# Layer 0 of a four-layer image network: Silu built from exp and ln, and its steps laid into separate slots

## The chip, the cores and the metric

The kernel runs on one core of a Trainium2 chip. The metric is the device time of one execution in microseconds (us). The core has five engines that run side by side: TensorE (PE, with its weight loads shown apart as PEld), VectorE (DVE), ScalarE (ACT), GpSimd (POOL) and the DMA queues (issued here by SP). Each engine works through its own instructions in order and waits for the others through semaphores.

## The reference

Four layers work one after the other on four images of 64 x 64 positions with 128 channels; each adds its result to its input. Only layer 0 is changed. Cut to what matters:

```python
xz = gn(x) @ in_proj_w.T                    # 128 -> 512 channels
xh, z = jnp.split(xz, 2, axis=-1)           # 256 each
z = jax.nn.silu(z)                          # silu(v) = v / (1 + exp(-v))
xc = depthwise_conv_3x3(xh)
xc = jax.nn.silu(xc + conv_b)
xs = [xc by rows, xc by columns, and both reversed]          # 4 directions
delta = softplus(dt_proj(x_proj(xs)) + dt_bias)              # ln(1 + exp(.))
for t in range(4096):                                        # 16 states n per channel
    h[n] = exp(delta[t] * A[n]) * h[n] + delta[t] * xs[t] * B[t, n]
    y[t] = sum_n h[n] * C[t, n]
y = sum over the 4 directions, plus D * xs
y = layernorm(y) * out_norm_w + out_norm_b
x = x + (y * z) @ out_proj_w.T
```

Layers 1 to 3 (Fourier layers and a neighbourhood attention) follow and are the same in both kernels.

## The kernel before

Layer 0 works image by image. An image has four directions of eight chunks (512 positions each), which makes 32 units; a unit has 16 slots, one for each state n. In a slot GpSimd makes dB = du * B, ScalarE makes dA = exp(delta * A) for the two halves s of the channels, VectorE runs the recurrence as two scans h, and TensorE transposes the h of seven slots earlier into pt; ScalarE copies that to hT, and TensorE multiplies it with W (made from C) into yT. During an image's units two further stages are fed piece by piece into the slots: `before` of the next image (norm, in_proj, conv, Silu) and `after` of the last image (layer norm, gate, out_proj, residual). The first image's `before` runs ahead of all units, as the opening, in an order that the compiler's scheduler chooses; in the units the written order is kept. The last image's `after` follows at the end.

```python
psx = pool("l0psx", 3, space=PSUM)      # 3 banks of dA, tag "x"
psm = pool("l0psm", 1, space=PSUM)      # 1 shared bank, tag "m"
exp_and_ln = lambda: nc.scalar.preload_act_table_set("natural_log_exp_and_others")
...
def before(b, bank, act, dve):
    ...                                 # 8 pieces: transposes and statistics of x
    s_, o_ = sh.group_scale(st, psm, small, "m")     # has a Sqrt
    exp_and_ln()
    for c in range(NCH):
        ...                             # transposes, norm into xn; in_proj xh, copied into pad
        for s in range(2):
            for t in range(9):
                if t % 3 == 0:
                    yield "c"
                if t == 0:
                    pm = bank("cv")
                dy, dx = divmod(t, 3)
                nc.tensor.matmul(pm, lhsT=taps[:, s, t, :],
                                 rhs=pad[:, s, dy : dy + 8, dx : dx + 64], ...)
            zp = psx.tile([P, CH], F32, name="zp", tag="x")
            nc.tensor.matmul(zp, lhsT=w_in[:, 2 + s, :], rhs=xn[:, o : o + CH], ...)
            act(lambda *a: gates(b, *a), c, s, pm, zp)

def gates(b, c, s, pm, zp):
    xo = tmp.tile([P, CH], F32, name="xo", tag="t2", bufs=4)
    nc.scalar.activation(xo, pm, AF.Silu, bias=conv_b[:, s : s + 1])
    ...                                 # DMA to xr
    xw = tmp.tile([P, 64, 8], F32, name="xw", tag="t2", bufs=4)
    nc.scalar.activation(xw, pm.rearrange("p (h w) -> p w h", w=64), AF.Silu, bias=...)
    ...                                 # DMA to xw
    z = tmp.tile([P, CH], F32, name="z", tag="t2", bufs=4)
    nc.scalar.activation(z, zp, AF.Silu)
    exp_and_ln()
    ...                                 # DMA to z
```

The slot loop, cut; `flush(act)` runs what a piece of an earlier slot has left for ScalarE, `flush(dve)` what it has left for VectorE:

```python
for n in range(NS):
    dB = ...;  nc.gpsimd.tensor_tensor(dB, du, B_now[...], ALU.mult)
    flush(dve)
    for s in range(2):
        dA = psx.tile([P, CH], F32, name="dA", tag="x")
        nc.scalar.activation(dA, delta[:, s, :], AF.Exp, scale=A_neg[:, k, s, n : n + 1])
        nc.vector.tensor_tensor_scan(h[:, s, :, q], dA, dB[:, s, :], state[...], ALU.mult, ALU.add)
        if s == 0:
            flush(act)
            ...                         # exp and ln of the next unit's delta at n = 8, 10
    copy = transposed()                 # PE: pt, then yT of the slot before
    copy()                              # ACT: hT <- pt
    if n in CRS:                        # CRS = {2: 0, 4: 1, 11: 2, 13: 3}
        cr = spare("cr");  nc.tensor.matmul(cr, ...);  defer(dve)(weights, ...)   # W <- cr
    ...
    # one piece of `before` or `after`; conv pieces start at n == 14 and go on in the next two slots
```

Of the kernel before, what the change touches and what calls it, by code (L numbers as in the profile page):

```python
# [16 lines left out]
P = 128  # L17
# [64 lines left out]
def layer0(sh, A, x_in, x_out, scr):  # L82
# [7 lines left out]
    with ExitStack() as ctx:  # L90
# [16 lines left out]
        on_w, on_b = cols[:, 28:30], cols[:, 30:32]  # L107
        w_x = wp.tile([P, 2, K4, 40], F32, name="w_x")
# [32 lines left out]
        def before(b, bank, act, dve):  # L141
# [4 lines left out]
            for c in range(NCH):  # L146
                yield "f"
                t = tmp.tile([P, 4, DM], F32, name="xs", tag="t2", bufs=4)
                nc.sync.dma_start(t, tiles(x_in(b)[c * CH : (c + 1) * CH, :]))
                yield "m"  # L150
                pt = bank("gn_ps")
                for q in range(4):
                    nc.tensor.transpose(pt[:, q * P : (q + 1) * P], t[:, q, :], sh.ident)
                dve(lambda c=c, pt=pt: nc.vector.bn_stats(st[:, c, :], pt))
# [3 lines left out]
            for c in range(NCH):  # L158
# [13 lines left out]
                for j in range(0, j1 - j0, 3):  # L172
# [3 lines left out]
                    for q in range(j, e):  # L176
                        nc.tensor.transpose(pt[:, (q - j) * P : (q - j + 1) * P], t[:, q, :], sh.ident)
                    dve(
                        lambda j=j, e=e, pt=pt: nc.vector.tensor_scalar(  # L179
                            xn[:, j * P : e * P], pt[:, 0 : (e - j) * P], s_, o_, ALU.mult, ALU.add  # L180
                        )
                    )
                for s in range(2):
                    for r in range(r0, r1, 5):
# [8 lines left out]
                        act(  # L193
                            lambda s=s, p0=p0, n=n, pm=pm: nc.scalar.copy(
                                pad[:, s, p0 : p0 + n, 1:65], pm[:, 0 : 64 * n].rearrange("p (h w) -> p h w", w=64)
                            )
                        )
                o = (8 * c - 2 * j0) * 64
                for s in range(2):
                    for t in range(9):  # L200
# [12 lines left out]
                    zp = psx.tile([P, CH], F32, name="zp", tag="x")  # L213
                    nc.tensor.matmul(zp, lhsT=w_in[:, 2 + s, :], rhs=xn[:, o : o + CH], start=True, stop=True)
                    act(lambda *a: gates(b, *a), c, s, pm, zp)

        def gates(b, c, s, pm, zp):

            xo = tmp.tile([P, CH], F32, name="xo", tag="t2", bufs=4)
            nc.scalar.activation(xo, pm, AF.Silu, bias=conv_b[:, s : s + 1])  # L220
            nc.sync.dma_start(scr(f"xr{b % 2}")[s, :, c * CH : (c + 1) * CH], xo)
            xw = tmp.tile([P, 64, 8], F32, name="xw", tag="t2", bufs=4)
            nc.scalar.activation(xw, pm.rearrange("p (h w) -> p w h", w=64), AF.Silu, bias=conv_b[:, s : s + 1])
            nc.sync.dma_start(scr(f"xw{b % 2}")[s].rearrange("p (w h) -> p w h", h=64)[:, :, 8 * c : 8 * c + 8], xw)
            z = tmp.tile([P, CH], F32, name="z", tag="t2", bufs=4)
            nc.scalar.activation(z, zp, AF.Silu)
            exp_and_ln()
            nc.sync.dma_start(scr(f"z{b % 2}")[s, :, c * CH : (c + 1) * CH], z)

        def after(b, st, bank, act, dve):  # L230
# [8 lines left out]
            for c in range(NCH):  # L239
# [3 lines left out]
                nc.sync.dma_start(y, tiles(scr("y2")[rows, :]))  # L243
                z = tmp.tile([P, 2, CH], F32, name="zf", tag="t4", bufs=4)
                nc.sync.dma_start(z, scr(f"z{b % 2}")[:, :, rows].rearrange("s p t -> p s t"))
# [8 lines left out]
                for s in range(2):  # L254
                    yield "m"
                    pt = bank("pg")
                    for q in range(4):
                        nc.tensor.transpose(pt[:, q * P : (q + 1) * P], y[:, q, s * P : (s + 1) * P], sh.ident)
                    act(
                        lambda s=s, yg=yg, pt=pt: nc.scalar.activation(  # L260
                            yg[:, s, :], pt, AF.Identity, scale=on_w[:, s : s + 1], bias=on_b[:, s : s + 1]
                        )
                    )
# [4 lines left out]
                yield "m"  # L268
                op = bank("op").rearrange("p (q d) -> p q d", q=4)
# [5 lines left out]
                dve(lambda *a: residual(b, *a), rows, xr, op)  # L275
# [53 lines left out]
        at_once = lambda f, *a: f(*a)  # L329
        for _ in before(0, any_bank, at_once, at_once):  # L330
# [88 lines left out]
        CRS = {2: 0, 4: 1, 11: 2, 13: 3}  # L419
        BUSY = (*CRS, 6, 7, 8, 9, 10)  # L420
        act, dve = [], []
        defer = lambda todo: (lambda f, *a: todo.append(lambda: f(*a)))

        def flush(todo):
            for f in todo:
                f()
            todo.clear()
# [10 lines left out]
        with tc.manual_schedule(engines=order):  # L438
            for i, (b, k, c) in enumerate(units):
                if i % per == 0:  # L440
                    ln_st = small.tile([P, NJ, 1, 6], F32, name="ln_st")
                    if b + 1 < NB:
                        sides.insert(0, Side(before(b + 1, spare, defer(act), defer(dve)), 113 + 8, NS * i, 29 * NS))
                rev = k >= 2
                pc = NCH - 1 - c if rev else c
                dst = lambda n, pc=pc: tiles(scr(f"y{n}")[pc * CH : (pc + 1) * CH, :])
# [7 lines left out]
                for n in range(NS):  # L454
                    g, q = divmod(n, 4)
# [10 lines left out]
                    flush(dve)  # L466
                    if i + 1 < len(units) and n in (9, 11):
                        next(coming)
                    for s in range(2):
# [5 lines left out]
                        if s == 0:  # L475
                            flush(act)
                            if i + 1 < len(units):
                                if n == 7:
                                    xd_next, bd_next = next(coming)
                                if n in (8, 10):  # L480
                                    next(coming)
                    copy = transposed() if NS * i + n >= LAG else (lambda: None)
                    copy()
                    if n == 1:
                        for f in ends.pop("state", []):
                            f()
                    if n in CRS:
                        cr = spare("cr")
                        nc.tensor.matmul(cr, lhsT=sel[:, CRS[n], :], rhs=xd[0:40, :], start=True, stop=True)  # L489
                        defer(dve)(weights, Ws, CRS[n], int(rev), cr)  # L490
# [11 lines left out]
                    if i + 1 < len(units):  # L502
                        if n == 3:
                            u_next, v_next = fetch(*units[i + 1])
                        if n == 6:
                            coming = inputs(*units[i + 1][1:], v_next)
                        if n in (6, 7, 9):
                            next(coming)
                        if n == 13:
# [11 lines left out]
                    holds = any(d.inside or d.run for d in sides)  # L521
# [1264 lines left out]
```

## Time and profile before

| | |
|---|---|
| time, median of 3 runs | 8981.49 us (8977.56 to 8983.19) |
| span of the profiled execution | 9002.5 us |
| PE / DVE / ACT / POOL busy over the span | 81% / 78% / 70% / 62% |
| opening, to the first scan | 222 us |
| images 0, 1, 2, 3 in the scan | 1592, 1618, 1618, 1447 us |
| ACT loads of a table of functions, in front of xo and by exp_and_ln | x49 and x58, 1283 ns each |
| scan h, 128x512 | x4096, mean 1270 ns |
| dA, 128x512 | x4096, mean 690 ns |
| hT <- pt, 128x1024 | x2048, mean 1011 ns |
| dB, 128x1024 | x2048, mean 2378 ns |

A line of the groups names the source line, the engine, the operation, the tile written and those read, the shapes and the count; then come the busy time, the mean of one, and the idle time of the engine just before it with what ended it. A line of the waits names who waited for whom, with the sum, the count and the longest. A line of the timeline gives start and length in us. Overlapping instructions of one engine are each counted from their own start to their own end, so that the mean of one can be somewhat longer than its share of the time.

### The profile page before, as it was taken

To read this page: it belongs to the slowest core of one execution; us is meant where nothing else is said; L and a number is where in the kernel's file an instruction comes from. 1 tells how busy PE (TensorE), PEld (TensorE's weight loads), DVE (VectorE), ACT (ScalarE), POOL (GpSimd) and SP (SyncE) were. 2 spreads that over 40 slices of the span, in tenths; PEclk is the share of its full clock that TensorE was granted. 3 is DMA by queue.
4 is the path that set the end of the run, shared out by engine and by line. 5 is a ranking of instruction groups with operands and counts; after the bars stand their busy time and mean duration, and the time that the engine had idled before them with its cause. 6 is when DMAs were issued, how large, how long until landed. Compare 5 with 4: busy or idle time off the path is not lost. (4 is left out here: it accounts for less than half of the span.)

```text
span 9002.5 us, 141536 instructions
## 1 busy us (share of the span) xinstructions
PE 7279.6 (81%) x54256; PEld 4342.6 (48%) x54256; DVE 6999.1 (78%) x8298; ACT 6266.3 (70%) x9869; POOL 5607.3 (62%) x2998
## 2 busy tenths in 40 slices
PE   8788888878888887888888778887768968488588
PEld 3344444444444444444444444444457745365366
DVE  1788888998889899898888999999824543534578
ACT  2788888888788788887888888888712212515467
POOL 0788888888878788887878888999700010110233
PEclk9799999999999999999999999999979978688699
DMA  6234544434454443444545333444341033240333
GB/s 108 99 121 138 132 124 141 126 122 133 129 135 139 138 131 118 128 135 123 147 138 135 123 122 136 146 139 140 111 104 47 24 93 100 75 118 30 90 90 87
DMA packets 1148650, 1037.91 MB, mean 115 GB/s; under 512 B 564127, under 2 KB 1001979, under 8 KB 1081156
## 3 DMA queue, kind: packets, MB, share of 16 engines
q1 hardware_dynamic: 1146292, 1027.13, 39.3%
q8 instruction: 426, 6.98, 0.3%
q14 instruction: 252, 2.06, 0.1%
q10 hardware_dynamic: 1680, 1.74, 0.1%
HBM read 845.18 MB, written 181.32 MB: 114 GB/s over the span
## 5 line engine op out<-in xcount | busy, mean ns | idle before, releaser
L465 POOL TENSOR_TENSOR dB<-du,Bb 128x1024 f32<-128x1024 f32 x2048 | 4841.1, 2378 | 974.4 <-DVE h L472 554.1
L472 DVE TENSOR_TENSOR_SCAN h<-dA,state,dB 128x512 f32<-128x512 f32 x4096 | 4972.6, 1270 | 507.3 <-ACT dA L471 428.8
L358 PE MATMUL pt<-ident,h 128*128 128x128 f32 x16384 | 2319.7, 287 | 868.2 <-ACT hT L368 856.5
L471 ACT ACTIVATE dA<-delta,A_neg 128x512 f32<-128x512 f32 x4096 | 2757.5, 690 | 250.3 <-DVE h L472 221.4
L358 PEld LDWEIGHTS pt<-ident,h 128*128 128x128 f32 x16384 | 1872.4, 145 | 2067.6 <-ACT hT L368 1744.5
L368 ACT COPY hT<-pt 128x1024 f32<-128x1024 f32 x2048 | 2070.6, 1011 | 540.4 <-PE pt L358 526.9
L393 PE MATMUL yT<-hT,W 128*32 128x256 f32 x16384 | 1364.2, 406 | 3.9 <-DVE y L409 3.3
L489 PE MATMUL cr<-xd,sel 40*128 40x512 f32 x1024 | 611.3, 678 | 39.1 <-DVE delta L310 20.3
L206 PE MATMUL cv<-pad,taps 128*128 128x512 f32 x1152 | 536.5, 606 | 7.3 <-DVE W L431 6.6
L393 PEld LDWEIGHTS yT<-hT,W 128*32 128x32 f32 x16384 | 328.3, 110 | 364.7 <-issue 351.2
L855 POOL TENSOR_TENSOR xg<-xg,so 128x1024 f32<-128x1024 f32 x8 | 26.5, 3337 | 695.4 <-ACT so L855 674.4
L1504 POOL TENSOR_TENSOR S<-S,sm 128x784 f32<-128x784 f32 x128 | 191.4, 1495 | 403.3 <-DVE sm L1502 341.7
L431 DVE TENSOR_TENSOR W<-cr,diag 128x512 f32<-128x512 f32 x512 | 343.5, 671 | 57.6 <-PE cr L489 57.0
L304 PE MATMUL dp<-xd,w_dt 65*128 65x512 f32 x512 | 294.7, 658 | 70.4 <-DVE delta L310 69.8
L313 POOL TENSOR_TENSOR du<-delta,u 128x1024 f32<-128x1024 f32 x128 | 304.4, 2378 | 73.3 <-DVE delta L310 73.3
L206 PEld LDWEIGHTS cv<-pad,taps 128*128 128x128 f32 x1152 | 206.0, 189 | 275.6 <-issue 259.6
L855 POOL TENSOR_TENSOR z<-z,sp 128x1024 f32<-128x1024 f32 x16 | 41.9, 2617 | 475.9 <-ACT z L855 475.6
L489 PEld LDWEIGHTS cr<-xd,sel 40*128 40x128 f32 x1024 | 160.5, 196 | 275.0 <-issue 134.0
L294 PE MATMUL xd_ps<-u,w_x 128*40 128x512 f32 x512 | 251.0, 613 | 40.9 <-DVE xn L179 21.1
L1511 ACT ACTIVATE S<-S,mx 128x196 f32<-128x196 f32 x512 | 228.2, 449 | 33.7 <-DVE mx L1538 33.3
L855 PE MATMUL pz<-PT,WX 128*68 128x64 f32 x2048 | 163.3, 244 | 94.4 <-DVE WX L855 76.6
L855 POOL TENSOR_TENSOR WX<-wr,Xs 128x544 f32<-128x544 f32 x32 | 45.1, 1408 | 269.4 <-DMA wr<-wt 239.4
(333 smaller groups left out, 7888.9 us busy)
## 6 DMA issues: line engine op xcount, KB each, us to landing
Bb<-l_B SPq DMA_DIRECT2D x512, 1024.0 KB
l_y<-y SPq DMA_DIRECT2D x128, 512.0 KB
wr<-wt SPq DMA_DIRECT2D x256, 136.0 KB
u<-l_xw SPq DMA_DIRECT2D x64, 512.0 KB
y<-l_y SPq DMA_DIRECT2D x64, 512.0 KB
u<-l_xr SPq DMA_DIRECT2D x64, 512.0 KB
V<-l_v SPq DMA_DIRECT2D x512, 49.0 KB
l_xr<-xo SPq DMA_DIRECT2D x64, 256.0 KB
```

The costliest lines, as they stand in the source:

```text
L206: nc.tensor.matmul(pm, lhsT=taps[:, s, t, :], rhs=pad[:, s, dy : dy + 8, dx : dx + 64], start=(t == 0), stop=(t == 8),)
L304: nc.tensor.matmul(dp, lhsT=w_dt[:, k, s * P : (s + 1) * P], rhs=xd, start=True, stop=True)
L313: nc.gpsimd.tensor_tensor(du, delta, u, ALU.mult)
L358: nc.tensor.transpose(pt[:, j, s, :], G["h"][:, s, t0 : t0 + 32, :].rearrange("p t n -> p (t n)"), sh.ident)
L368: return lambda: nc.scalar.copy(hT, pt.rearrange("p j s d -> p j (s d)"))
L393: nc.tensor.matmul(U["yT"][e][32 * jo : 32 * jo + 32, qo % 2, :], lhsT=U["Ws"][G["g"]][:, 4 * q + j, :], rhs=hT[:, j, :], start=((e, jo) n ...
L431: nc.vector.tensor_tensor(W, cr.rearrange("p (a t) -> p a t", t=32), diag[:, rev : rev + 1, :].to_broadcast([P, 16, 32]), ALU.mult,)
L465: nc.gpsimd.tensor_tensor(dB, du, B_now[:, q : q + 1, :].to_broadcast([P, 2, CH]), ALU.mult)
L471: nc.scalar.activation(dA, delta[:, s, :], AF.Exp, scale=A_neg[:, k, s, n : n + 1])
L472: nc.vector.tensor_tensor_scan(h[:, s, :, q], dA, dB[:, s, :], state[:, s, n : n + 1], ALU.mult, ALU.add)
L489: nc.tensor.matmul(cr, lhsT=sel[:, CRS[n], :], rhs=xd[0:40, :], start=True, stop=True)
L855: r = f(*args, **kw)
```

## The change

Silu has a set of functions of its own in ScalarE's tables, and exp and ln are in another, which must be loaded again afterwards. The changed kernel computes silu(v) as v * exp(-ln(1 + exp(-v))): exp, ln and exp on ScalarE from the set that the scan uses anyway, and a product on VectorE. The two copies of the conv's Silu, by rows and by columns, are now one Silu and a copy of it. Work left over by a piece gets a place in a given later slot: "dve" at its start, "act0" and "act1" behind the first and the second dA, "act2" behind the copy of pt. The z matmul gets a piece of its own ("z", at n = 12), two slots ahead of its group's conv.

As the shared bank is now held longer by conv and z, the matmuls of `after` (pg and op) take a bank of dA, in pieces "x" at n = 4, 6, 8 or 10, and the slots of cr and of the inputs of the next unit move. Scratch z has three copies instead of two and y2 two instead of one, so that `after` may spread over 28 units instead of 22.

```diff
-                    zp = psx.tile([P, CH], F32, name="zp", tag="x")
-                    nc.tensor.matmul(zp, lhsT=w_in[:, 2 + s, :], rhs=xn[:, o : o + CH], start=True, stop=True)
-                    act(lambda *a: gates(b, *a), c, s, pm, zp)
 (ahead of the conv of the same s)
+                    yield "z"
+                    zp = bank("zp")
+                    nc.tensor.matmul(zp, lhsT=w_in[:, 2 + s, :], rhs=xn[:, o : o + CH], start=True, stop=True)
+                    silu(zp, 0.0, 0.0, scr(f"z{b % 3}")[s, :, c * CH : (c + 1) * CH], later, (0, 0, 1))
 (behind the conv)
+                    bias = conv_b[:, s : s + 1], conv_nb[:, s : s + 1]
+                    xo = silu(pm, *bias, scr(f"xr{b % 2}")[s, :, c * CH : (c + 1) * CH], later, (0, 1, 2))
+                    later("act0", by_columns, xo, scr(f"xw{b % 2}")[s], c, slots=4)
...
-        def gates(b, c, s, pm, zp):      (three Silus and exp_and_ln, shown above)
+        def silu(v, bias, minus, dst, later, wait):
+            e = tmp.tile([P, CH], F32, name="e", tag="t2", bufs=4)
+            def product():
+                nc.vector.scalar_tensor_tensor(e, v, bias, e, ALU.add, ALU.mult)
+                nc.sync.dma_start(dst, e)
+            later("act0", nc.scalar.activation, e, v, AF.Exp, scale=-1.0, bias=minus)
+            later("act1", nc.scalar.activation, e, e, AF.Ln, bias=1.0, slots=1 + wait[0])
+            later("act0" if wait[1] else "act2", nc.scalar.activation, e, e, AF.Exp, scale=-1.0, slots=1 + wait[1])
+            later("dve", product, slots=1 + wait[2])
+            return e
+        def by_columns(xo, dst, c):
             xw = tmp.tile([P, 64, 8], F32, name="xw", tag="t2", bufs=4)
+            nc.scalar.copy(xw, xo.rearrange("p (h w) -> p w h", w=64))
...
 (in after; op likewise)
-                    yield "m"
-                    pt = bank("pg")
+                    yield "x"
+                    pt = psx.tile([P, CH], F32, name="pg", tag="x")
...
-        CRS = {2: 0, 4: 1, 11: 2, 13: 3}
-        BUSY = (*CRS, 6, 7, 8, 9, 10)
+        CRS = {3: 0, 4: 1, 10: 2, 11: 3}
+        BUSY = (*CRS, 5, 6, 7, 8, 9)
...
-                    sides.insert(0, Side(before(...), 113 + 8, NS * i, 29 * NS))
+                    sides.append(Side(before(...), 17 + 8 * 15, NS * i, 29 * NS))
...
-                sides = [Side(after(...), 4 + 8 * 6, NS * (i + 1) + 8, 22 * NS)]
+                sides = [Side(after(...), 4 + 8 * 7, NS * (i + 1) + 8, 28 * NS)]
```

In the opening, `later` runs each step where it is written, and all banks, zp's too, come in turn from the three of dA and the shared one.

## The prediction

> **What bounds the kernel now.** I first cut the span into stretches, at the scans that begin each image of layer 0, and asked for the busy time of every engine in each: opening, images 0 to 3, and the tail of image 3. The columns are stretch and length, then PE, PEld, DVE, ACT and POOL busy (instructions), then clock and DMA.
>
> ```profile
> 0.00:222.00 222.00, 181.35 (x476) 85.51 (x476) 25.25 (x60) 60.02 (x100) 7.03 (x27) 0.93 0.62 109
> 222.00:1814.00 1592.00, 1333.29 (x9192) 713.68 (x9192) 1389.56 (x1321) 1330.45 (x1836) 1298.10 (x680) 0.94 0.44 126
> 1814.00:3432.00 1618.00, 1354.20 (x9490) 736.75 (x9490) 1447.29 (x1400) 1327.34 (x1847) 1315.73 (x687) 0.96 0.46 132
> 3432.00:5050.00 1618.00, 1356.94 (x9490) 738.19 (x9490) 1447.71 (x1400) 1328.13 (x1847) 1315.62 (x687) 0.96 0.46 132
> 5050.00:6497.00 1447.00, 1163.44 (x9016) 647.07 (x9016) 1417.73 (x1367) 1244.00 (x1725) 1306.24 (x665) 0.97 0.38 132
> 6497.00:6615.00 118.00, 59.70 (x300) 44.42 (x296) 21.59 (x80) 22.02 (x26) 18.73 (x8) 0.63 0.33 102
> ```
>
> The last image, which prepares no next image, is bound by VectorE: 1417.73 of 1447 us. Images 1 and 2 have only 30 us more VectorE work but take 171 us more; VectorE stands idle there for 1618 - 1447 = 171 us each (202 in image 0). The list of VectorE's waits within 222 to 6497 says on whom:
>
> ```profile
> DVE h L472 <- ACT dA L471: 428.8, 334, 4.6
> DVE W L431 <- PE cr L489: 57.0, 50, 1.8
> ```
>
> So the loss is exponentials (dA) that come late from ScalarE. The timeline around one of the 48 conv groups inside the scan shows why (start, length, engine, instruction, idle time before it and its releaser):
>
> ```profile
> 4137.09 2.84 PE L206 MATMUL cv<-pad,taps 128*128 128x512 f32 x6
> ...
> 4138.38 2.46 DVE L472 TENSOR_TENSOR_SCAN h<-dA,state,dB 128x512 f32<-128x512 f32 x2 [1.07 <-POOL pad L166]
> ...
> 4141.30 2.84 PE L206 MATMUL cv<-pad,taps 128*128 128x512 f32 x6
> 4141.81 0.70 ACT L471 ACTIVATE dA<-delta,A_neg 128x512 f32<-128x512 f32 x1
> ...
> 4142.52 1.28 ACT L220 ACT_TABLE_LOAD   x1
> 4142.60 1.28 DVE L472 TENSOR_TENSOR_SCAN h<-dA,state,dB 128x512 f32<-128x512 f32 x1 [1.77 <-ACT dA L471]
> ...
> 4144.18 0.69 ACT L220 ACTIVATE xo<-cv,cols 128x512 f32<-128x512 f32 x1 [0.38 <-PE cv L206]
> ...
> 4145.95 1.28 ACT L119 ACT_TABLE_LOAD   x1
> ...
> 4147.25 0.69 ACT L471 ACTIVATE dA<-delta,A_neg 128x512 f32<-128x512 f32 x1
> ...
> 4147.97 1.28 DVE L472 TENSOR_TENSOR_SCAN h<-dA,state,dB 128x512 f32<-128x512 f32 x1 [4.09 <-ACT dA L471]
> ...
> 4148.94 1.43 PE L358 MATMUL pt<-ident,h 128*128 128x128 f32 x8 [2.49 <-ACT hT L368]
> ```
>
> Two losses sit side by side. The conv's three pieces of 2.84 us stretch three slots to the 4.2 us that TensorE needs (start to start of these two pieces: 4141.30 - 4137.09), against some 2.7 without them (1447/512 = 2.83 is the mean slot of image 3, with its other work). Then load, three Silus and load keep dA away from 4142.51 to 4147.25. After it TensorE is slow: the transposes take 1.43 us here and 1.97 us two slots on, against 1.04 before. Over all 48 groups, from the starts of the scans in the trace, the slots from one before the loads to two after take 18.5 us, and the same four slots of image 3 take 10.6: 7.9 us per group, 127 us per image. That is most of the 171.
>
> **What the Trainium skill says.** "ScalarE: Activation LUTs", section "What ACT_TABLE_LOAD costs", gives about 1283 ns for a load and 1380 ns more for a drain. The trace agrees on the load (1.28 us) but shows no second part: the load at 4145.95 ends at 4147.23 and dA starts at 4147.25. I count 1.28. The same page, "Table sets: the hidden batching unit", says that natural_log_exp_and_others holds both exp and ln; after the first few units the trace indeed has no load between the two activations of delta. "TensorE: Matmul & The Clock Gate", section "What's actually happening", says an idle window of about 3.4 us halves the clock. The 2.49 us gap above, shorter than that, already comes with longer matmuls, so the tendency agrees and the threshold isn't confirmed.
>
> **The change, part by part.**
>
> *Removed in the scan.* 48 groups lose two loads (48 x 2 x 1.28 = 123 us of ScalarE) and three Silus (688 + 681 + 598 ns in the groups by form, 1.97 us each group).
>
> *Added in the scan.* Each group gets six activations of about 0.6 us (the exp and ln of delta, same shape, are 596 and 632 ns) and one copy of about 0.6: 4.2 us. That is no less than the 4.5 removed; the gain must come from the spread. VectorE gets two products of 663 ns (the row of delta's SCALAR_TENSOR_TENSOR): 1.3 us per group, 64 us in all.
>
> *The group replayed by hand*, on the timeline above. The conv ends at about 4144.0, as before, so the waits of 1.07 and 1.77 stay. exp (0.69) runs from 4144.2 and dA follows at 4144.8, ends at 4145.5: the scan waits 1.6 us and not 4.09. ln, then the copy of the transposes, then dA of the next slot end at 4147.6: another 0.9 us. The second exp hides. At the end of slot 2 I am at 4150.1 and before was at 4152.0. The product adds 0.66. Before, the next W then waited 1.4 us for a slowed cr matmul (2.07 us for the two); that wait goes. At the first scan of the next slot: before 4154.0, after 4150.75 plus one W of 0.67, so 2.6 us gained. The z chain, three activations in slot 13, costs ScalarE 1.85 us where it has 0.4 to 1.2 idle per slot; its product falls into waits that the conv makes anyway. I charge 0.2. **Net 2.4 us per group, 115 us for 48.**
>
> *Opening.* Here the change adds loads. In the instruction order of the changed kernel on ScalarE, 64 loads stand in the opening, each ln and each exp after it bringing its own set: the preload after the group scale has no instruction that depends on it and no longer stands in front of them. The kernel before has one load for all Silus there. Per chunk: four chains of 0.6 + 1.28 + 0.63 + 1.28 + 0.6 = 4.4 us, two copies and four pad copies (2.0): 20.8 us of ScalarE. TensorE needs 21.06 us per chunk (conv to conv: 55.63, 76.69 in the timeline of xo) and was nearly alone:
>
> ```profile
> 55.63 0.69 ACT L220 ACTIVATE xo<-cv,cols 128x512 f32<-128x512 f32 x1 [7.59 <-PE cv L206]
> ...
> 76.69 0.69 ACT L220 ACTIVATE xo<-cv,cols 128x512 f32<-128x512 f32 x1 [7.66 <-PE cv L206]
> ```
>
> Now the pad copies of a chunk stand behind the last chain of the chunk before, about 6 us after its conv, and one xh matmul waits for the bank which that chain holds until its product. The next conv starts about 8 us after the last instead of 4, and starts with a slowed TensorE, about 1 us more. 5 us x 8 chunks = 40, plus the longer last chain before the first fetch: **+43 us.** Further, 16 loads in the first units of image 0 (8 in front of ln, 8 in front of dA) stay as they are.
>
> *The later stage.* pg and op take dA's banks, 24 times an image in three images. For one slot dA then has two banks and not three; one dA takes 0.69 us and a scan 1.2, so two are enough. The opposite sign is possible too, since pg no longer waits for the single shared bank. I count 0. In the tail (118 us, 8 chunks) the second pg no longer waits 0.8 us for the first: **-6 us.** The third z and the second y2 only widen the time in which the stage may run; VectorE shows no wait for these transfers, so 0.
>
> Sum: -115 + 43 - 6 = -78; 8981 - 78 = 8903, rounded to 8905.
>
> **The rivals.** (a) *All of the gate was a stall*: the 7.9 us per group shrink to the conv's own 3 or so, and two products are hidden: about 4.5 us per group, -216, net 8800. For it: nearly all of VectorE's idle time names dA. Against it: dA behind a conv is late through TensorE too. (b) *VectorE becomes the payer*: its 64 us of products add in full, and spread activations still delay dA, since ScalarE has just 0.45 us of slack in a 2.7 us slot (two dA and a copy, 2.25). Then 0 to -40 in the scan, the opening costs 43, and the total is 8980 to 9025. For it: image 3 is 98% VectorE. Against: in the group's slots VectorE is the one that waits. (c) *The opening is worse*, with ScalarE at 20.8 us per chunk as the bound and TensorE cold at every start: +70 and not 43. (d) *dA's lost bank bites*: 72 uses x 0.7 us = 50 us in images 1 to 3. Image 3 alone would show it.
>
> **Range and chances.** The scan's term has the width: -40 to -200. The opening is +25 to +70. 8810 to 8990 holds most combinations. Faster by over 2% (under 8802) needs rival (a) whole: 0.11. Slower by over 2% (over 9161) needs something I don't see: 0.03. Within 2%: 0.86.
>
> **What would show it.** Opening: first scan at about 265 us instead of 222, with 64 loads on the line of the new calls. Images 1 and 2: about 1580 us each instead of 1618, VectorE busy about 20 us more, its wait for dA near 300 us instead of 429. Image 3 unchanged at 1447 within 10 (else rival d). Loads in the scan: 8 + 8 + 6 pairs' worth and no Silu. Transposes after a conv back at 1.04 us. I am wrong if the conv's own slots shrink as well, as then the 1.07 and 1.77 us waits were the gate's, or if the opening doesn't lengthen.

## The result and the profile after

The changed kernel takes **9038.48 us** (median of 4 runs, 9027.3 to 9051.41); the kernel before, in the same comparison, 8982.34 (4 runs, 8977.56 to 8994.99). The ratio is 1.0061 with a 95% interval of 1.0041 to 1.008: slower by 0.6%, within the 2%, where the prediction had 8905 and a range that ended at 8990.

The stretches of the changed kernel follow, cut as before at the first scan of each image and the last scan: opening, images 0 to 3, and the tail up to the last residual. The columns are stretch and length, then PE, PEld, DVE, ACT and POOL busy (instructions), then clock, DMA share and GB/s.

```profile
0.00:272.70 272.70, 197.47 (x476) 92.86 (x476) 47.87 (x94) 183.91 (x225) 7.15 (x28) 0.87 0.48 89
272.70:1833.70 1561.00, 1303.40 (x9192) 700.59 (x9192) 1408.76 (x1353) 1320.47 (x1868) 1297.51 (x679) 0.96 0.41 129
1833.70:3448.70 1615.00, 1345.66 (x9490) 733.90 (x9490) 1468.79 (x1432) 1321.78 (x1879) 1313.89 (x687) 0.96 0.42 132
3448.70:5063.40 1614.70, 1347.52 (x9490) 734.76 (x9490) 1468.97 (x1433) 1321.78 (x1879) 1314.11 (x687) 0.96 0.42 132
5063.40:6538.60 1475.20, 1164.99 (x9016) 650.25 (x9016) 1425.88 (x1368) 1245.92 (x1725) 1304.69 (x665) 0.97 0.38 129
6538.60:6642.90 104.30, 54.97 (x296) 42.24 (x296) 20.64 (x78) 21.00 (x26) 18.70 (x8) 0.69 0.37 114
```

Beside the kernel before, with its cuts set at the same events (222.1, 1813.8, 3431.9, 5049.9, 6497.2, 6611.1):

| stretch | before, us | after, us | difference |
|---|---|---|---|
| opening | 222.1 | 272.7 | +50.6 |
| image 0 (prepares image 1) | 1591.7 | 1561.0 | -30.7 |
| image 1 (prepares 2, finishes 0) | 1618.1 | 1615.1 | -3.0 |
| image 2 (prepares 3, finishes 1) | 1618.0 | 1614.6 | -3.4 |
| image 3 (finishes 2) | 1447.3 | 1475.2 | +27.9 |
| tail | 113.9 | 104.3 | -9.6 |

The gain is only in image 0, where no later stage runs. Image 3, where nothing of Silu runs, lost as much. ScalarE's busy time in the opening went from 60 to 183.91 us, of which the new calls' line of loads has 83.4.

A caution on sums: the stretches add to +31.8, the two whole profiled executions differ by 22 (9002.5 and 9024.5), the timed medians by 56. The layers behind the tail, the same in both kernels, vary by some 20 us over the runs of this study, and the profiled execution of the kernel before was 22 us above its median. The images repeat better (image 0 lies between 1561.0 and 1563.9 in all runs that leave it and the loads alone), so **the experiments are read from the stretches**, and the timed ratio only where several rounds were run. Most stretches are of one trace each: image 3, left alone, took 1475.1, 1475.2, 1476.4 and once 1481.0 us, and image 1 took 1608.8 and 1618.3 in two kernels that are alike up to there. A single difference of a few us is therefore no finding.

The waits of VectorE from 273 to 6539 us (who waited for whom, sum in us, times, longest):

```profile
DVE h L492 <- ACT dA L491: 356.1, 335, 4.6
```

The wait for dA fell from 428.8 to 356.1 only, still with a longest of 4.6 us. In image 3 alone it rose from 17.8 us (34 times) to 33.6 (53 times). The timeline of the changed kernel at the same place of a conv group, here in image 0:

```profile
1063.43 2.84 PE L214 MATMUL cv<-pad,taps 128*128 128x512 f32 x6
...
1064.73 1.28 DVE L492 TENSOR_TENSOR_SCAN h<-dA,state,dB 128x512 f32<-128x512 f32 x1 [1.77 <-ACT dA L491]
...
1066.31 0.69 ACT L437 ACTIVATE e<-cv,conv_nb 128x512 f32<-128x512 f32 x1 [1.68 <-PE cv L214]
1066.89 0.69 ACT L491 ACTIVATE dA<-delta,A_neg 128x512 f32<-128x512 f32 x1
...
1067.51 0.62 ACT L437 ACTIVATE e<-e 128x512 f32<-128x512 f32 x1
1067.61 1.28 DVE L492 TENSOR_TENSOR_SCAN h<-dA,state,dB 128x512 f32<-128x512 f32 x1 [1.60 <-ACT dA L491]
...
1069.08 1.09 PE L368 MATMUL pt<-ident,h 128*128 128x128 f32 x8 [1.36 <-ACT hT L378]
...
1069.72 2.47 DVE L492 TENSOR_TENSOR_SCAN h<-dA,state,dB 128x512 f32<-128x512 f32 x2 [0.82 <-ACT dA L491]
...
1072.10 0.72 DVE L230 SCALAR_TENSOR_TENSOR e<-cv,cols,e 128x512 f32<-128x512 f32 x1
```

The wait of 4.09 us behind load, three Silus and load is now 1.60 and then 0.82; the wait of 1.77 at the middle piece of the conv stayed; the transposes take 1.09 us where they took 1.43.

### The profile page after: what moved, and what is told of

It is laid out like the page before. It is cut to its first block, busy times and chain, and to the rows that moved or that the text cites. A ratio compares the mean times of both kernels' runs of the same rounds, so it can differ in the third digit from the quotient of the medians.

```text
span 9024.5 us, 141918 instructions
## 1 busy us (share of the span) xinstructions
PE 7237.4 (80%) x54256; PEld 4329.0 (48%) x54256; DVE 7091.2 (79%) x8427; ACT 6368.6 (71%) x10090; POOL 5601.5 (62%) x2998
## 5 line engine op out<-in xcount | busy, mean ns | idle before, releaser
L492 DVE TENSOR_TENSOR_SCAN h<-dA,state,dB 128x512 f32<-128x512 f32 x4096 | 4972.6, 1267 | 431.3 <-ACT dA L491 356.1
L368 PE MATMUL pt<-ident,h 128*128 128x128 f32 x16384 | 2293.0, 285 | 882.9 <-ACT hT L378 874.7
L305 PE MATMUL xd_ps<-u,w_x 128*40 128x512 f32 x512 | 254.7, 621 | 29.9 <-DMA u<-l_xw 21.1
L876 PE MATMUL pz<-PT,WX 128*68 128x64 f32 x2048 | 165.8, 247 | 92.1 <-DVE WX L876 76.1
L318 ACT ACTIVATE delta<-dp 128x512 f32<-128x512 f32 x256 | 153.6, 600 | 117.4 <-PE dp L315 115.3
```

What stands on the lines that cost most here:

```text
L368: nc.tensor.transpose(pt[:, j, s, :], G["h"][:, s, t0 : t0 + 32, :].rearrange("p t n -> p (t n)"), sh.ident)
L876: r = f(*args, **kw)
```

## The experiments

**Theory at the start.** Silu's own gain is real, as image 0 shows, and three costs eat it: the loads of the opening, the later stage's new places, and the moved slots of cr and of the next unit's inputs. **Rivals.** The opening is longer because of its order and banks, not its loads; VectorE pays for the products; the lost bank of dA alone makes image 3 longer. Seventeen further kernels were run. Where one leaves out or changes what is computed, the text says so.

### The opening: one set for the whole of layer 0

```diff
-        self.nc.scalar.activation(r, var, AF.Sqrt, bias=self.eps5[: shape[0]])   # and a reciprocal
+        self.nc.scalar.activation(r, var, AF.Ln, bias=self.eps5[: shape[0]])     # in layer 0 only
+        self.nc.scalar.activation(r, r, AF.Exp, scale=-0.5)
-            exp_and_ln()     # behind each group scale and each rstd; now once, at the very start
```

> Changed kernel, but in layer 0 both reciprocal roots are exp(-0.5 ln(var + eps)), so that no Sqrt leaves the set of exp and ln: one table load stands in the whole of layer 0. Theory 'loads': the opening (to the first scan) falls from 272.7 us to about 235, since 64 loads of 1.28 us go from a ScalarE chain on which the next chunk's pad copies wait; the first four units of image 0 fall from 55 to about 46 us each (16 loads), images 1 to 3 stay within 6 us (two loads twice per image). In all about 75 us less than the changed kernel, near 8965. Rival 'order and banks': pad copies behind the chains and the bank held by the conv make the opening long, loads or not: the opening stays above 255.

The opening took 224.5 us: 48 less than in the changed kernel, 2 more than before. ScalarE's timeline of one conv chain, in the changed kernel (start, length):

```profile
74.53 0.67 ACT L340 ACTIVATE e<-cv,conv_nb 128x512 f32<-128x512 f32 x1
75.22 1.28 ACT L340 ACT_TABLE_LOAD   x1
76.51 0.63 ACT L340 ACTIVATE e<-e 128x512 f32<-128x512 f32 x1
77.16 1.28 ACT L340 ACT_TABLE_LOAD   x1
78.45 0.63 ACT L340 ACTIVATE e<-e 128x512 f32<-128x512 f32 x1
```

and with one set (ln and exp stand in one row):

```profile
65.05 0.69 ACT L343 ACTIVATE e<-cv,conv_nb 128x512 f32<-128x512 f32 x1 [2.86 <-PE cv L218]
65.77 1.29 ACT L343 ACTIVATE e<-e 128x512 f32<-128x512 f32 x2
```

A chain of 4.6 us became one of 2.0. So all of the opening's loss but 2 us goes away with the loads; banks, order and products, which the edit leaves as they were, cost next to nothing once the chains are short. With the loads in place they are the path on which the chains reach TensorE. Its xh matmuls in the opening, in the changed kernel and in the kernel before:

```profile
L192 PE MATMUL xh<-xn,w_in 128*128 128x320 f32 (+1 forms) x64 | 31.8, 644 | 32.0 <-DVE xn L182 22.6 <-ACT pad L198 6.9 <-DVE e L230 2.5
```

```profile
L189 PE MATMUL xh<-xn,w_in 128*128 128x320 f32 (+1 forms) x64 | 20.8, 472 | 6.5 <-DVE xn L179 4.8 <-ACT z L226 1.7
```

TensorE waits 25.5 us longer, above all for xn, which VectorE makes behind products that themselves wait for ScalarE's chains (186.2 us in 32 waits). Its xh and zp matmuls take 15.4 us longer (31.8 and 20.7 us against 20.8 and 16.3), and the first x_proj waits 8.9 us longer for its fetch (21.1 against 12.2): 49.8 of the 50.6 us. The kernel without the products, below, bears the path out: with all 65 loads in place the wait for xn falls from 22.6 to 5.3 us and the opening to 259.4.

The 16 loads in the first units of image 0 went too, and image 0 fell from 1561.0 to 1526.1, all of it in its first four units: 35 us for loads that take 16 x 1.28 = 20.5. What the other 14 us waited for was not followed. Images 1 to 3 moved little (1608.8, 1607.6, 1475.1). Timed: 8939.38 against 9001.26, ratio 0.9932, interval 0.9915 to 0.995. With this one repair the change is a gain of 0.7%, but the loss in image 3 is still all there.

### Image 3: which of the moved parts costs

Three kernels put back one part of the old arrangement each, in image 3 only. The old slots of cr:

```diff
-                if n in CRS:                        # 3, 4, 10, 11
+                crs = {2: 0, 4: 1, 11: 2, 13: 3} if b == NB - 1 else CRS
+                if n in crs:
```

> Changed kernel, but in the units of the last image cr stands in slots 2, 4, 11, 13 as in the kernel before, not in 3, 4, 10, 11. Image 3 took 1475 us in the changed kernel and 1447 before. Theory 'pairs' (two cr in neighbouring slots on the one shared bank: the second waits until VectorE has made the first W, and TensorE stands and cools): image 3 falls to 1450 to 1458. Theory 'lent bank' (pg and op on dA's banks): it stays at 1470 to 1478. Theory 'place' (pieces of after at n = 4 to 10, beside the inputs of the next unit): stays too.

The shared bank for pg and op, so that dA keeps its three:

```diff
-                    yield "x"
-                    pt = psx.tile([P, CH], F32, name="pg", tag="x")      # op likewise
+                    yield "m" if shared else "x"
+                    pt = spare("pg") if shared else psx.tile([P, CH], F32, name="pg", tag="x")
```

> Changed kernel, but the later stage that runs in image 3 takes the shared bank for pg and op, in free slots (0 to 2, 12 to 15), as in the kernel before; cr stays in 3, 4, 10, 11. Theory 'lent bank': image 3 falls from 1475 to about 1450. Theory 'pairs': it stays at 1468 or more. Theory 'place': it falls to about 1450 as well, and the run with other slots on dA's banks tells the two apart.

And the pieces of the later stage in slots where the inputs' work does not stand, with the bank of dA:

```diff
-                            at = dict(f=True, x=n in (4, 6, 8, 10), ...)
+                            at = dict(f=True, x=n in ((0, 1, 2, 12, 13, 14, 15) if b == NB - 1 else (4, 6, 8, 10)), ...)
```

> Changed kernel, but in image 3 pg and op, still on dA's banks, stand in slots 0 to 2 and 12 to 15 instead of 4, 6, 8, 10. Theory 'place': image 3 falls from 1475 to about 1452. Theories 'lent bank' and 'pairs': it stays within 8 us of 1475.

Then the first two together, the same with the later stage over 22 units instead of 28, and that with the inputs of the next unit (x_proj, delta's exp and ln) one slot later and their fetch two slots later, as before the change:

```diff
+                old = int(b == NB - 1)
-                    if i + 1 < len(units) and n in (8, 10):
+                    if i + 1 < len(units) and n - old in (8, 10):        # and so for each of their slots
```

> Changed kernel with both measures for the last image: cr in slots 2, 4, 11, 13, and pg and op on the shared bank in free slots. Alone they gave 1467.8 and 1461.9 us for image 3, from 1475.2. If the causes are separate, the gains add: 7 + 13, image 3 at 1453 to 1457. If both mend the same wait, it stays at 1460 or more.

> The same, and the stage spread over 22 units as in the kernel before, not 28. If lent bank, place, pairs and spread are all there is, image 3 returns to the 1447 us of the kernel before, within 4. If something else in the changed kernel's slots costs time (the inputs of the next unit one slot earlier), it stays above 1452.

> Changed kernel; in image 3 everything stands as in the kernel before: pg and op on the shared bank, cr in 2, 4, 11, 13, the stage over 22 units, and now the matmuls of the next unit's inputs one slot later (6, 7, 9 instead of 5, 6, 8) too. With the first three image 3 took 1457.1 us. If the slots of the inputs are the last cause, it returns to 1447 within 3. If it stays at 1455 or more, something that is no slot (the place of deferred work behind copies, the scratch) costs the last 10.

| put back in image 3 | image 3, us | against 1475.2 |
|---|---|---|
| slots of cr | 1467.8 | -7.4 |
| shared bank | 1461.9 | -13.3 |
| slots of the later stage's pieces | 1471.1 | -4.1 |
| cr and bank | 1459.6 | -15.6 |
| cr, bank, 22 units | 1457.1 | -18.1 |
| the same and the inputs | 1444.9 | -30.3 |

No part is the whole. The bank bites, but not for all 28 us: the shared bank also brings the pieces into the other slots, which alone are worth 4.1, so the bank itself is about 9 (1471.1 - 1461.9). Cr and bank overlap (15.6 together, where their sum is 20.7). The 4.1 of the slots and the 2.5 of the 22 units are no larger than differences that come without any edit. **The largest step left, 12.2 us, is the inputs' slots**, which the theories pairs, lent bank and place had left out. By directions it is no simple gain: the units of the second and third direction win 5 and 14 us and those of the first lose 7. With all put back image 3 is slightly below its old 1447.3, so the list holds the whole loss; how large each part is may depend on the order in which they are put back.

### Silu alone: loads, spread and product

To see what the loads and Silu's own set cost the kernel before, Silu was replaced there by Exp, without loads. This kernel computes something else in the gate, with the same number of instructions.

```diff
-            nc.scalar.activation(xo, pm, AF.Silu, bias=conv_b[:, s : s + 1])     # xw and z likewise
-            exp_and_ln()
+            nc.scalar.activation(xo, pm, AF.Exp, bias=conv_b[:, s : s + 1])
```

> Kernel before, with exp in the place of every Silu and no load behind it (the sigmoid is left out, so that the outputs are other ones): the groups keep three activations in one place and lose their two loads. Image 0 took 1591.7 us before and 1561.0 in the changed kernel; the 13 slots around a group 44.3 and 41.7. Theory 'loads are the whole of the gate': a group falls by more than the changed kernel's 2.7, to about 40.5 (2.6 us of loads and a TensorE that stays at speed), image 0 to 1540 or less. Theory 'activations as well': three activations of 2 us in one place hold dA up, the group stays at 41.7 or above, image 0 at 1558 or more.

Images 0, 1 and 2 took 1539.8, 1568.7 and 1573.1 us: 52, 49 and 45 less than before, for 32 loads of 1.28 us = 41 us in each. The opening, whose Silus had one load in all, stayed at 222.2, and image 3, which has no gate, at 1447.3. That is the most that taking away the gates' loads is worth in this arrangement, and the changed kernel found 31, 3 and 3. Around a conv group (13 slots, from the starts of the scans in the trace, mean over image 0) the kernel before takes 44.31 us, this one 41.12 and the changed one 41.65: in image 0 most of it was found inside the group, and the rest was lost outside. In images 1 and 2, where the later stage runs too, it was not: the same 13 slots take 44.82 and 45.20 us before, 44.48 and 44.40 in the changed kernel, a gain of 0.3 and 0.8 only. (Windows shifted by up to three slots give 2.4 to 3.4 for image 0 and 0.3 to 2.1 for the other two.)

The reverse: the changed kernel with exp, ln and exp of a Silu behind one dA instead of in slots of their own (the product and the copy by columns follow two slots later).

```diff
-            later("act1", nc.scalar.activation, e, e, AF.Ln, bias=1.0, slots=1 + wait[0])
-            later("act0" if wait[1] else "act2", nc.scalar.activation, e, e, AF.Exp, scale=-1.0, slots=1 + wait[1])
+            later("act0", nc.scalar.activation, e, e, AF.Ln, bias=1.0)
+            later("act0", nc.scalar.activation, e, e, AF.Exp, scale=-1.0)
```

> Changed kernel, with the exp, ln and exp of a group all behind the first dA of one slot instead of three places, the product one slot later. If the spread is what makes the chain cheap, dA waits 1.25 us more at each conv and the 13 slots around a group take 42.5 to 43 us instead of 41.7, image 0 about 1575 to 1582. If ScalarE has to catch up anyway, with the same work in the same units, image 0 stays within 4 us of 1561.

The group takes 45.33 us, image 0 1623.2, images 1 and 2 1663.3 and 1658.8; its wait for dA over the scan:

```profile
DVE h L492 <- ACT dA L491: 453.0, 448, 4.6
```

The same instructions without any load, bunched, are 32 us slower than the kernel *before* in image 0 and 41 to 45 in the two others. That is three to four times the cost expected. The spread, not the missing loads alone, makes this Silu usable; as z's chain, the product and the copy moved with it, which of them costs most is not shown.

Last the two products of a group, left out (the Silu is then the sigmoid alone):

```diff
-                nc.vector.scalar_tensor_tensor(e, v, bias, e, ALU.add, ALU.mult)
```

> Changed kernel without the products v * e on VectorE (the factor v of silu is left out, so that the outputs are other ones). 32 products of 0.7 us stand in image 0. My step: the product of z falls into waits that the conv makes anyway, that of the conv adds 0.66: image 0 falls from 1561 to about 1548 to 1553. If VectorE pays for both in full, it falls to 1541 or less; if both are hidden, it stays above 1557.

Image 0 stayed where it was (1563.0), against the 8 to 13 us expected; images 1 and 2 fell to 1594.7 and 1597.6, by 20 and 17 us; 32 products of 727 and 677 ns are 22.5 us per image. So the products are free in image 0, where VectorE waits anyway, and are paid nearly in full in images 1 and 2, where VectorE carries the later stage too. There the 13 slots of a group fall to 43.18 us, by 1.2 to 1.3.

### Silu and the later stage apart

The same edit on both kernels takes the later stage out of the images; all four run behind the last unit, on scratch that other images have by then partly overwritten, so what they compute is not the reference's, and only the four images of the scan are read.

```diff
-                    sides = [Side(after(b, ln_st, ...), ...)]
+                    sides = []
+                    if b == NB - 1:
+                        sides = [Side(after(o, ln_st, ...), ...) for o in range(NB)]
```

> Kernel before, with the later stage of all four images after the last unit (its inputs are then overwritten scratch, so the outputs are other ones): images 1 and 2 carry only the preparation of the next image, as image 0 does, but without image 0's 16 loads in the first units. Image 1 and 2 near 1557 each (1592 less the 35 that one set took off image 0). Image 3 near 1395.

> Changed kernel, edited in the same way. If the Silu change brings 31 us in every image and the later stage's new place costs 28 (sum of parts), images 1 and 2 are near 1526, 31 below those of the kernel before edited so, and image 3 is near 1395 in both. If the Silu change brings less in images 1 and 2 by itself, they stand above 1540.

| us | before alone | after alone | Silu and moved slots | later stage, before | later stage, after |
|---|---|---|---|---|---|
| image 0 | 1591.5 | 1563.3 | -28.2 | - | - |
| image 1 | 1549.6 | 1523.0 | -26.6 | 68.5 | 92.1 |
| image 2 | 1549.7 | 1522.5 | -27.2 | 68.3 | 92.1 |
| image 3 | 1374.9 | 1395.8 | +20.9 | 72.4 | 79.4 |

The later stage's cost is the image with it minus the image without it, in the same arrangement. This is the ledger that the prediction lacked. Silu with its slots is worth 27 us in images 1 and 2 as well; the later stage **takes 24 us of it back in each**, and 7 in image 3. Silu's part is near the 31 expected. But image 3, expected at 1395 in both, is so in the changed kernel alone: with neither Silu nor later stage, 20.9 us are lost to moved slots. The wait for dA there is 4.8 us in the kernel before (this edit) and 23.4 in the changed one, the first line below and the second:

```profile
DVE h L472 <- ACT dA L471: 4.8, 16, 0.4
```

```profile
DVE h L492 <- ACT dA L491: 23.4, 33, 1.9
```

The timeline of the changed kernel, later stage taken out, shows such a place in image 3:

```profile
5033.14 0.60 ACT L318 ACTIVATE delta<-dp 128x512 f32<-128x512 f32 x1
5033.77 0.63 ACT L319 ACTIVATE delta<-delta 128x512 f32<-128x512 f32 x1
...
5034.92 0.58 ACT L417 COPY y<-yT 128x512 f32<-128x512 f32 x1
5035.40 1.01 ACT L378 COPY hT<-pt 128x1024 f32<-128x1024 f32 x1
...
5036.46 1.89 PE L368 MATMUL pt<-ident,h 128*128 128x128 f32 x8 [1.97 <-ACT hT L378]
...
5042.67 1.29 DVE L492 TENSOR_TENSOR_SCAN h<-dA,state,dB 128x512 f32<-128x512 f32 x1 [1.29 <-ACT dA L491]
```

Moved one slot earlier, delta's exp and ln (1.23 us) meet the copy of y out of yT (0.58) in one slot, ahead of the copy of the transposes; in the kernel before that copy of y stood one slot ahead of them. From 5033.14 to 5036.41 ScalarE works without a break, 3.3 us, where a slot of this image takes 1395.8 / 512 = 2.73. TensorE waits 1.97 us for hT and its next transposes take 1.89 us; of the scans that follow three wait for dA, by 0.50 and 0.54 us and, behind the second exp and ln, by 1.29. Two kernels test it: the old slots of cr in image 3, and the copy of y one slot later in the one direction where it meets the inputs:

```diff
+                    if k == 1:
+                        later("act0", taken_out)       # nc.scalar.copy(ye, yT), and the DMA of y after the fourth
```

> The changed kernel with the later stage taken out of the images, and cr back in slots 2, 4, 11, 13 in image 3 only. Image 3, which carries nothing but its own units, took 1395.8 us with the moved slots and 1374.9 in the kernel before edited alike. If the moved cr costs the 21 us, image 3 falls to 1377 or less; if the inputs of the next unit, one slot earlier, cost them, it stays within 4 of 1396.

> The changed kernel with the later stage taken out, and in the units of the first direction ScalarE's copy of y out of yT one slot later, behind the next slot's first dA. In the changed kernel that copy (0.58) stands in slot 7 together with the exp and ln of delta that moved there from slot 8; the copy of the transposes comes late, TensorE stands 2 us and its next matmuls take 1.9 us instead of 1.1. If this meeting is the cost, the eight units of the first direction in image 3 fall from 44.3 to 43.4 us each or below; units of the other directions stay. If not, they stay at 44.3.

Cr gives back 3.7 of the 20.9 us (1392.1), the copy of y 10.9 (1384.9; the units of that direction go from 44.3 us to 43.1). Images 0, 1 and 2 gain 5, 4 and 4 from the copy of y. But the meeting is not half of the cost, as the traces show by directions: the 20.9 us are 7.5, 2.6, 10.6 and 0.2 from the first to the last. The copy of y out of yT by ScalarE stands in the first direction alone, so the meeting can be 7.5 us at most, and the later copy wins more than that (the first direction's units took 43.4 us in the kernel before). In the last version below it wins 4 us in image 3's first direction with the inputs in their old slots, where the two had not met. Of the third direction's 10.6 us cr is 3.8; the rest was not taken apart.

### A version that beats both

Put together: one set for layer 0 and image 3 in its old arrangement.

> The changed kernel with one set of functions in all of layer 0 (reciprocal roots by exp and ln) and, in image 3, the arrangement of the kernel before. One set alone took 62 us off the kernel before (ratio 0.9932). The arrangement adds 18 to 28: 0.9905 to 0.9915 of the kernel before, near 8915.

8908.67 against 8996.48, ratio 0.99, interval 0.9884 to 0.9917, about as expected. Then a thing that the traces had shown on the way: yf, the normalisation in the later stage, waits on VectorE for GpSimd. It was moved to ScalarE:

```diff
+            nc.vector.scalar_tensor_tensor(nm, mv[:, :, 0], -1.0, rs, ALU.mult, ALU.mult)
-                    nc.vector.tensor_scalar(y[:, q, :], y[:, q, :], mv[:, j, 0:1], rs[:, j : j + 1], ALU.subtract, ALU.mult)
+                    nc.scalar.activation(y[:, q, :], y[:, q, :], AF.Identity, scale=rs[:, j : j + 1], bias=nm[:, j : j + 1])
```

> The same, and the layer norm of the later stage (yf) on ScalarE as scale and bias, not on VectorE. On VectorE each yf lasts 0.38 us where GpSimd is idle, but 2.1 us in the median, ending with GpSimd's dB: 50 us per image. If it waits for GpSimd there, VectorE is rid of those 50 us in images 1 to 3 and ScalarE gets 16 us per image: 60 to 120 us less than best1. If it is only slow by itself, or ScalarE is as tight as VectorE, under 30 us less.

8760.29, ratio 0.9733, interval 0.9718 to 0.9747: 148 us less, where 60 to 120 were expected. Images 1, 2 and 3 fell by 57, 49 and 41 us (1618.3, 1611.7, 1440.6 to 1561.2, 1563.0, 1399.9; the first is 48 against the 1608.8 of the kernel with one set). So nearly all of the 50 us that yf held VectorE in each image came out. With the later copy of y:

> The version with one set of functions, the old arrangement in image 3 and yf on ScalarE (ratio 0.9733), with y's copy one slot later in the units of the first direction. Images 0 to 2 have the moved inputs: 8 us less in each if the meeting in slot 7 is the cost, ratio 0.970 to 0.972. No change if it isn't.

8745.85 against 9004.26, ratio 0.9712, interval 0.9696 to 0.9728. Images 0 to 2 are 6, 5 and 6 us shorter, where 8 were expected, and image 3, whose inputs had not moved, 4. It is the fastest version; its lead over the one before it lies within the intervals.

## Why the prediction was wrong

**The step that failed is a term that was not in the sum.** "Net 2.4 us per group, 115 us for 48" was taken as the whole of the scan. Nothing was charged for the moved slots of cr and of the inputs, although the diff names them. They cost 20.9 us in image 3, where nothing else of the change stands once the later stage is out. In images 0 to 2 they can only be inferred. With the later stage out of both kernels, a group gains 2.59, 2.47 and 2.46 us there, which is 41, 40 and 39 us per image, and the images gain 28, 27 and 27: 12 to 13 us go elsewhere in each. As 16 groups of 13 slots cover 208 of 512 slots, 20.9 x 304 / 512 = 12.4 would fall outside them, so the moved slots fit, if they cost the same in every image. That is not shown: the one part measured in all four, the copy of y, gives 11 us in image 3 and 4 to 5 in the others. Over four images it is about 59 us.

**"I count 0" for the later stage** was the second failure: 23.6, 23.8 and 7.0 us, 54 in all. Rival (d), the lost bank, is part of it: about 9 us in image 3, and 13.3 with the slots that go with it. "One dA takes 0.69 us and a scan 1.2, so two are enough" looked at the mean; that the third bank is what ScalarE works ahead into when it is late is likely, but no trace was read for it. The prediction named its own test (image 3 within 10 of 1447), and +27.9 failed it, but the bank was less than half of that. In images 1 and 2 the loss sits around the conv, where a group gains 0.3 and 0.8 us and not 2.4. The largest part that a run shows there is the products: left out, they give 20 and 17 us in these images and nothing in image 0. How the rest divides between bank, slots and the wider spread was not separated.

**"+43" for the opening** measured +50.6, within its bounds, and the loads were its root, 64 of them counted rightly (65 are on their line). The path was another, so that the size is partly luck. The prediction let TensorE wait 4 us per chunk for pad copies behind the chain and for a held bank; in the wait at xh these are 6.9 and 2.5 us in all, and 22.6 are xn on VectorE, behind products that wait for the chains, of which the prediction says nothing. The slowed TensorE, charged with 8 us, is up to 15. Rival (c), +70, did not come true.

**The group's own gain was right where no later stage runs.** 2.66 us in image 0 against 2.4, and slot by slot: the waits in the trace above are 1.77, 1.60 and 0.82 us, where the replay by hand had 1.77, 1.6 and 0.9. Rival (a), that all of the gate was a stall, fell: the wait of 1.77 at the conv's middle piece stayed. Two sizes in it were off: the copy by columns takes 1.107 us, not "about 0.6", and the conv's product, charged with 0.66, costs nothing in image 0. The group's total came out all the same.

**Rival (b)** was right by half: the products are hidden in image 0 and cost 17 to 20 us in images 1 and 2. Its band for the scan, 0 to -40, holds the measured -9, but with products as the whole cause it would be luck: they are 37 of the 106 us that are missing. The charge for VectorE of about 20 us busy per image was right (1468.79 against 1447.29).

**The tail** gave -9.6 instead of -6.

In sum for the scan: -115 predicted, -9 found. With the later stage out, Silu and the moved slots give -28.2, -26.6, -27.2 and +20.9, together -61; the later stage takes 54 back, which leaves -7, and image 0 was 2.5 us better in the one trace than in the other. The -61 are -120 from the groups and 59 from elsewhere, of which 20.9 are measured. With opening and tail the stretches end at +32; the timed difference of 56 has some 24 us more, which are not explained.

## What to carry to other kernels

A change that takes work off a slot is priced with everything that it moves to make room: for each moved operation, add up ScalarE's work in the slot where it arrives, not the mean of the loop. Work that is free in one stage (the products in image 0) can be paid in full in another that carries more. A stage without the changed operation (image 3 here) shows that side cost alone, and it is worth asking the trace for the busy time of such slots before predicting. Where several functions share a set, a stray Sqrt is worth an exp and ln of its own, since one set for a whole layer took 48 us from the opening and 35 from the first image.

## What the runs showed of the hardware

*VectorE waits for GpSimd within an instruction.* The later stage's tensor_scalar on 128x256, in image 3 of the changed kernel (after the count: minimum, median and maximum in ns):

```profile
L264 DVE TENSOR_SCALAR yf<-yf,ln_mv,ln_r x32: 381/2145/3377, 5195.4 to 6280.1; 128x256 f32<-128x256 f32 x32
```

and on ScalarE, in the second of the combined versions:

```profile
L269 ACT ACTIVATE yf<-yf,ln_nm,ln_r x128: 586/594/621, 1885.7 to 6351.9; 128x256 f32<-128x256 f32 x128
```

It takes 0.38 us at best and 2.1 in the middle, and no wait is shown: the time is inside the instruction, so VectorE counts as busy. The timeline of the kernel with one set shows two of them:

```profile
5424.88 7.08 POOL L488 TENSOR_TENSOR dB<-du,Bb 128x1024 f32<-128x1024 f32 x3 [1.56 <-DVE h L495]
...
5429.35 2.77 DVE L267 TENSOR_SCALAR yf<-yf,ln_mv,ln_r 128x256 f32<-128x256 f32 x2
```

GpSimd's dB ends at 5431.96, the pair of yf at 5432.12. Of the 68 yf of that trace that start while a dB runs, 65 end 0.1 to 0.4 us behind that dB and the other three as closely behind the next one; of the 28 that start between two, 19 take at most 0.4 us. The Trainium skill, "SBUF — State Buffer", section "Who interferes with whom", names tensor_scalar among the operations of VectorE that can take the port pair it shares with GpSimd, for the whole instruction, and says that ScalarE never waits for it. The trace agrees on both: 594 ns on ScalarE with a maximum of 621. My first reading, that "image 3 is 98% VectorE" and therefore bound by its work, took such blocked time for work; moving yf made image 3 41 us shorter.

*A load has nothing behind it.* In the opening of the changed kernel the load at 75.22 ends at 76.50 and ln starts at 76.51.

*The order of reading costs ScalarE.* The copy by columns reads e from SBUF with a step:

```profile
L241 ACT COPY xw<-e 128x512 f32<-128x512 f32 x48 | 53.1, 1107 | 4.0 <-DVE e L230 4.0
```

1107 ns, against 625 for ln and exp of the same size in order, and against 681 for the same order read from PSUM by the Silu before. The operations differ too (a copy, an activation), but the copy of y, of the same size and in order, takes 0.58 us.

*TensorE can slow after a short pause.* In image 3 of the changed kernel without the later stage, after 1.97 us without a matmul, the eight transposes took 1.89 us, against 1.04 to 1.09, and the granted clock was 0.50 from 5036.6 to 5040.0. It is no fixed rule. In the traces of both kernels, with and without the later stage, 12 of 2966 such groups took over 1.3 us after a pause of 0.5 to 1.8 us, 86 of 167 after 1.8 to 2.5 and 57 of 63 after a longer one.
